# Two-layer convolution-attention block on Trainium2: the order of 128-row and five-row score products in a tile's attention

## The chip, the cores and the metric

The kernel runs on one core of one Trainium2 chip, in one launch. The metric is the device time of that launch in microseconds (us), the median of several runs. The core's engines are named as the profile names them: PE is TensorE (PEld its weight loads), DVE is VectorE, ACT is ScalarE, POOL is GpSimd, SP is SyncE. PE writes its results into PSUM[...]; DVE and ACT read them from there.

## The reference, cut to what matters

The input `x` is fp32 of shape (2, 256, 64, 64): two images of 256 channels. Layer 0 is group norm, an eight-head attention over all 4096 pixels, and a residual. Layer 1 is group norm, then the sum of a grouped 3x3 convolution and of two local attentions in a row, and a residual. The change is in the first of these two attentions. Cut down, it is:

```python
q = conv1x1(x, conv1_w, conv1_b); k = conv1x1(x, conv2_w, conv2_b); v = conv1x1(x, conv3_w, conv3_b)
pos = tile(conv1x1(loc, convp_w, convp_b))        # loc: two coordinates of each pixel
fq = q * 64 ** (-0.5) + pos
fk = k + pos
# blockify: pixels with the same place inside their 8x8 block form a group; 64 groups an image,
# 64 pixels and 256 channels a group
att = softmax(einsum('bcn,bcm->bnm', blockify(fq), blockify(fk)) * 256 ** (-0.5))
ctx = einsum('bnm,bcm->bcn', att, blockify(v))
feats = relu(conv1x1(ctx, lr_W_w) * scale + shift)
```

The score of a query pixel n and a key pixel m in a group is a product over the 256 channels of `fq` and `fk`. Multiplied out, it has a part that contracts the input with itself through one folded 256x256 matrix, and parts that contain `pos` or a bias. The latter depend on few numbers for each pixel.

## The kernel before, in words

`tile_two_layer_kernel` calls `direct_layers`, which does all the work for one image (b = 0) and then for the other (b = 1). For each image it runs `project0` and `attention0` (layer 0), `layer1_first` (the first attention of layer 1, the subject here) and `layer1_second` (the second attention, `group_attention` again, and the convolution in between).

`layer1_first` first writes the normalised image into `xg`, in the order of groups. The 64 groups are cut into eight tiles t of eight groups, 512 pixels each; `source(t)` is that piece of `xg`, two chunks (c) of 128 channels by 512 pixels. For each tile there is:

- `project` (L1176, ACT copy at L1180): the tile multiplied by the folded matrix, `py`, copied to `y`. It runs two tiles ahead.
- `at_grid` (L1190, DVE at L1195 and L1198), twice an image: five rows for each pixel that hold the position and bias parts, as `queries` and `keys`. Tile t uses five rows from row 32 * (t % 4) of half t // 4.
- `group_attention`, a generator with the tile's softmax. It makes the values `vs` (L1060), and the scores `sp` (L1078 and L1084). `sp` is one PSUM bank: 128 partitions, four blocks of 64 columns. Block t of the inner loop, for `par` 0 and 1, holds group 4 * par + t on partitions 64 * par to 64 * par + 63. A group's scores are the sum of two products of 128 rows (c = 0 and 1: `y` against `xg`, L1078) and one product of five rows (`queries` against `keys`, L1084). Then DVE takes the row maximum (`nm`, L1094) and subtracts it (L1096), ACT takes the exponential (L1097), DVE the row sum, its reciprocal and the scaling (L1099 to L1101). After the first `yield`, PE transposes the result (`at`, L1106) and DVE spreads it into `bd` (L1115); after the second, PE multiplies it with the values (`pc`, L1124) and ACT writes `feats` (L1137).

The second attention calls the same function with `more=None`: its scores have only the 128-row products, 16 a tile.

The order on PE is written by hand (`tc.manual_schedule(engines={E.PE})`): the scores and values of tile t come first, then half the projection of tile t + 2, the transposes of tile t - 1, the other half, and the products `pc` of tile t - 1. In the last two tiles, which have nothing left to project, the generator stops once more behind the scores, and the transposes of tile t - 1 follow directly. The order on the other engines in this part is the planner's.

Beside the first image's attention DVE makes the convolution's weights in `conv_weights` (L888 to L936, tiles named `prep`): a long chain of scale-and-add steps of 128x256 (L917), in two halves. The second half's input `wx` is loaded by POOL's queue (L909) into room that the first half frees. The results go to memory from SP's queue (L930), and `fetch_conv_weights` loads them back as `wf` (L946) for the first convolution in `layer1_second`, where PE transposes them (L955). ACT fills `xp`, the padded image for the convolution, at the end of the stage (L1295), and POOL transforms it (`col`, L982, and `v`, L986) for the convolution's products (`mm`, L996).

Of the kernel before, what the change touches and what calls it, by code (L numbers as in the profile page):

```python
# [22 lines left out]
KC = C // P  # L23
# [17 lines left out]
def direct_layers(ctx: ExitStack, tc: tile.TileContext, a: dict, out: bass.AP, bad: bass.AP):  # L41
# [3 lines left out]
    nc = tc.nc  # L45
# [13 lines left out]
    def w4(shape, name, dtype=F32):  # L59
        return work.tile(shape, dtype, tag="w4", name=name)  # L60

    def bank(shape, name):
        return psum["ps"].tile(shape, F32, tag="bank", name=name)
# [983 lines left out]
    def group_attention(nm, q, k, tokens, wv, out, busy=False, apart=False, more=None, between=None):  # L1047

        vs = w4([P, 4, C], f"vs_{nm}")

        def values(half):
            pv = bank([P, 2, C], f"pvs_{nm}_{half}")
            for i in range(2):
                for c in range(KC):
                    nc.tensor.matmul(  # L1060
                        pv[:, i, :], tokens(c, 2 * half + i), wv[:, c, :], start=c == 0, stop=c == KC - 1
                    )
            dst = vs[:, 2 * half : 2 * half + 2, :]
            if half == 0 or busy or apart:
                nc.scalar.copy(dst, pv)
            else:
                nc.vector.tensor_copy(dst, pv)

        first = apart or more and more[2]
        if first:  # L1070
            values(0)

        sp = bank([P, 4, 64], f"sp_{nm}")
        for t in range(4):
            for c in range(KC):
                for par in range(2):
                    n0 = (4 * par + t) * 64
                    nc.tensor.matmul(  # L1078
                        sp[64 * par : 64 * par + 64, t, :], q[:, c, n0 : n0 + 64], k[:, c, n0 : n0 + 64],
                        start=c == 0, stop=not more and c == KC - 1,  # L1080
                    )
            for par in range(2 if more else 0):
                n0 = (4 * par + t) * 64
                nc.tensor.matmul(  # L1084
                    sp[64 * par : 64 * par + 64, t, :], more[0][:, n0 : n0 + 64], more[1][:, n0 : n0 + 64], start=False, stop=True
                )
        if more and more[3]:
            yield
        if not first:
            values(0)  # L1090
        if not apart:
            values(1)
        nm4 = small.tile([P, 4], F32, tag="nm4", name=f"nm4_{nm}")
        nc.vector.tensor_reduce(nm4, sp, AX.X, ALU.max, negate=True)  # L1094
        e = small.tile([P, 4, 64], F32, tag="e", name=f"e_{nm}")
        nc.vector.tensor_tensor(e, sp, nm4.unsqueeze(2).to_broadcast([P, 4, 64]), ALU.add)  # L1096
        nc.scalar.activation(e, e, AF.Exp, scale=SC1)  # L1097
        den = small.tile([P, 4], F32, tag="den", name=f"den_{nm}")
        nc.vector.tensor_reduce(den, e, AX.X, ALU.add)  # L1099
        nc.vector.reciprocal(den, den)  # L1100
        nc.vector.tensor_tensor(e, e, den.unsqueeze(2).to_broadcast([P, 4, 64]), ALU.mult)  # L1101

        yield
        at = bank([P, 2, 2, 64], f"at_{nm}")
        for u in range(2):
            nc.tensor.transpose(  # L1106
                at[:, u].rearrange("p a i -> p (a i)"),
                e[:, 2 * u : 2 * u + 2, :].rearrange("p t j -> p (t j)"), ident,
            )

        bd = bds[turn[0] % 2]
        turn[0] += 1
        for tt in range(2):
            rows = slice(64 * tt, 64 * tt + 64)
            nc.vector.tensor_copy(  # L1115
                bd[rows, :, tt, :].rearrange("p (a u) i -> p u a i", a=2), at[rows]
            )
        if apart:
            values(1)
        yield  # L1120
        for m in range(KC):
            pc = bank([P, T], f"pc_{nm}_{m}")
            for w in range(4):
                nc.tensor.matmul(  # L1124
                    pc[:, w * P : (w + 1) * P], vs[:, w, m * P : (m + 1) * P],
                    bd[:, w].rearrange("p a i -> p (a i)"), start=True, stop=True,
                )
            out(m, pc)
            if m == 0 and between:
                between()  # L1130
# [11 lines left out]
    def layer1_first(b, xts, put, check, st):  # L1142
# [102 lines left out]
        with tc.manual_schedule(engines={E.PE}):  # L1245

            before = None
            for t in range(NT + 1):
                parts = None
                if t < NT:  # L1250
                    def to_feats(m, pc, t=t):
                        kept["feats"] = bn_relu(
                            feats[m][:, :, t, :].rearrange("p o e -> p e o"),
                            pc.rearrange("p (e o) -> p e o", e=8), V_LR, m,
                        )

                    rows = slice(HD0 * (t % 4), HD0 * (t % 4) + AT)
                    parts = group_attention(
                        f"lr_{b}_{t}", tiles.pop(t), source(t),
                        lambda c, w, t=t: source(t)[:, c, w * P : (w + 1) * P], wts["w3"], to_feats, b == 0,  # L1260
                        more=(queries[rows, t // 4, :], keys[t // 4][rows, :], t == 0, t >= NT - 2),
                    )
                    next(parts)
                    if t == 3:
                        at_grid(1)
                for m in range(KC):
                    if t + 2 < NT:
                        project(t + 2, m, slice(1 if t == 0 else 0, KC))
                    if before:
                        next(before, None)  # L1270
                    if m == 0 and NT - 2 <= t < NT:
                        next(parts)
                before = parts
# [5 lines left out]
    def layer1_second(b, xts, feats, mean, rstd, shift, pacc, following):  # L1279
# [59 lines left out]
        for t in range(NT):  # L1339
# [25 lines left out]
            with tc.manual_schedule(engines={mybir.EngineType.PE}):  # L1365
# [17 lines left out]
                def to_res(m, pc, res=res):  # L1383
# [4 lines left out]
                    )  # L1388

                parts = group_attention(  # L1390
                    nt, q, k, lambda c, w, f=f: f[c][:, w * P : (w + 1) * P], wts["fv"], to_res, apart=t + 1 < NT,
                    between=lambda: next(then) if b == 0 and t == NT - 1 else None,
# [630 lines left out]
```

## Time and profile before

| | |
|---|---|
| median of three runs | 3069.78 us (3066.59 to 3073.84) |
| the profiled execution's own time | 3067.66 us |
| its span | 3065.9 us |
| PE busy | 2986.3 us (97%) |
| DVE busy | 2456.4 us (80%) |
| ACT busy | 2340.4 us (76%) |
| POOL busy | 832.6 us (27%) |
| score products of 128 rows in the first attention (L1078, `sp_lr`) | 512 records, first at 1161.5 us, last at 2761.1 us |
| score products of five rows (L1084, `sp_lr`) | 256 records, first at 1161.9 us, last at 2761.4 us |

The span is what the profiler saw of the program. The first attention stands at about 1161 to 1248 us for the first image and at about 2684 to 2771 us for the second. The profile writes `_lr` behind the names of the tiles of the first attention and `_sr` behind those of the second. A line of the timeline gives the start, the length, the engine, the line of the kernel, the operation, what is written from what, the shape, the number of records merged (x8), and in brackets the idle time of the engine before it and who ended it. The ends of PE's records are modelled and overlap the next starts, so the distance from start to start tells more than the length.

### The profile page before, as it was taken

To read this page: it belongs to the slowest core of one execution; us is meant where nothing else is said; L and a number is where in the kernel's file an instruction comes from. 1 tells how busy PE (TensorE), PEld (TensorE's weight loads), DVE (VectorE), ACT (ScalarE), POOL (GpSimd) and SP (SyncE) were. 2 spreads that over 40 slices of the span, in tenths; PEclk is the share of its full clock that TensorE was granted. 3 is DMA by queue.
4 is the path that set the end of the run, shared out by engine and by line. 5 is a ranking of instruction groups with operands and counts; after the bars stand their busy time and mean duration, and the time that the engine had idled before them with its cause. 6 is when DMAs were issued, how large, how long until landed. Compare 5 with 4: busy or idle time off the path is not lost. (4 is left out here: it accounts for less than half of the span.)

```text
span 3065.9 us, 63941 instructions
## 1 busy us (share of the span) xinstructions
PE 2986.3 (97%) x25129; PEld 1863.2 (61%) x25129; DVE 2456.4 (80%) x3122; ACT 2340.4 (76%) x3266; POOL 832.6 (27%) x918
## 2 busy tenths in 40 slices
PE   7999999999999999999989999999999999999998
PEld 4565566665556556677755655566555565576765
DVE  4698998989899999856556989989989999835543
ACT  2699999999999983622227999999999999734333
POOL 1122222222223240155301222322222222306440
PEclk9999999999999999999999999999999999999999
DMA  7968789787897661220159688797788976700000
GB/s 259 278 133 179 153 161 177 152 167 161 172 185 160 141 135 32 86 118 28 45 195 271 129 177 163 159 182 145 172 166 170 183 147 128 169 4 4 21 15 22
DMA packets 244148, 425.01 MB, mean 139 GB/s; under 512 B 98888, under 2 KB 109948, under 8 KB 241660
## 3 DMA queue, kind: packets, MB, share of 16 engines
q0 software_dynamic: 94720, 237.57, 40.1%
q1 hardware_dynamic: 148972, 182.99, 21.6%
q8 instruction: 199, 3.26, 0.4%
q14 instruction: 113, 0.93, 0.1%
q10 hardware_dynamic: 144, 0.26, 0.0%
HBM read 119.55 MB, written 68.39 MB: 61 GB/s over the span
## 5 line engine op out<-in xcount | busy, mean ns | idle before, releaser
L551 ACT ACTIVATE es<-ring 128x512 f32<-128x512 f32 (+2 forms) x1572 | 1203.4, 904 | 29.6 <-PE ring L545 21.7
L545 PE MATMUL ring<-q,k 128*128 128x512 f32 x4096 | 1082.3, 407 | 10.1 <-ACT v L551 4.8
L597 DVE TENSOR_TENSOR e<-e,es 128x1024 f32<-128x1024 f32 (+1 forms) x956 | 1035.3, 1144 | 23.1 <-ACT es L551 22.6
L545 PEld LDWEIGHTS ring<-q,k 128*128 128x128 f32 x4096 | 733.7, 188 | 379.8 <-ACT es L551 114.5
L551 ACT ACTIVATE v<-ring 128x512 f32<-128x512 f32 (+2 forms) x1024 | 780.7, 899 | 23.7 <-PE ring L545 12.8
L560 PE MATMUL av<-es,v 128*32 128x256 f32 (+1 forms) x9684 | 725.9, 389 | 0.0
L597 DVE TENSOR_TENSOR e<-e,v 128x1024 f32<-128x1024 f32 (+1 forms) x636 | 669.3, 1107 | 20.3 <-ACT v L551 19.3
L560 PE MATMUL av<-v 128*32 128x256 f32 (+1 forms) x6188 | 497.9, 389 | 0.0
L560 PEld LDWEIGHTS av<-es,v 128*32 128x32 f32 x9684 | 328.0, 110 | 266.1 <-issue 106.4
L560 PEld LDWEIGHTS av<-v 128*32 128x32 f32 x6188 | 221.2, 109 | 170.8 <-issue 72.4
L996 PE MATMUL mm<-v,wf 128*128 128x256 f32 x1024 | 227.6, 380 | 1.5 <-DVE z L1005 1.5
L607 POOL DMA_DIRECT2D es<-es x118 | 100.7, 853 | 465.7 <-ACT es L551 418.1
L996 PEld LDWEIGHTS mm<-v,wf 128*128 128x128 f32 x1024 | 193.3, 190 | 36.9 <-issue 9.9
L986 POOL TENSOR_TENSOR v<-col 128x512 f32<-128x512 f32 x128 | 165.4, 1319 | 177.7 <-ACT rk_sr L1137 39.3
L1001 ACT COPY z<-mm 128x512 f32<-128x512 f32 x32 | 18.7, 586 | 182.7 <-PE mm L996 182.7
L607 POOL DMA_DIRECT2D acc<-es x118 | 118.4, 1009 | 112.4 <-ACT es L551 49.3
L605 POOL DMA_DIRECT2D es<-es x20 | 11.4, 569 | 491.8 <-ACT es L551 405.6
L607 POOL DMA_DIRECT2D es<-v x72 | 61.4, 852 | 290.4 <-ACT v L551 278.0
L1002 DVE TENSOR_TENSOR z<-z,mm 128x512 f32<-128x512 f32 x32 | 22.0, 687 | 138.5 <-ACT z L1001 138.1
L607 POOL DMA_DIRECT2D v<-es x112 | 115.0, 1027 | 19.3 <-ACT es L551 11.2
L607 POOL DMA_DIRECT2D acc<-v x78 | 74.6, 957 | 78.1 <-DMA acc<-es 30.9
L982 POOL TENSOR_TENSOR col<-xp 128x1152 f32<-128x1152 f32 x32 | 69.6, 2175 | 62.1 <-DVE xp L1415 50.8
(254 smaller groups left out, 2680.0 us busy)
## 6 DMA issues: line engine op xcount, KB each, us to landing
acc<-es POOLq DMA_DIRECT2D x128, 512.0 KB, 6.4
acc<-v POOLq DMA_DIRECT2D x84, 512.0 KB, 6.2
es<-es POOLq DMA_DIRECT2D x138, 256.0 KB, 4.3
v<-es POOLq DMA_DIRECT2D x132, 256.0 KB, 5.2
k<-wk_halves SPq DMA_DIRECT2D x64, 512.0 KB
q<-wq_halves SPq DMA_DIRECT2D x256, 128.0 KB
v<-v POOLq DMA_DIRECT2D x90, 256.0 KB, 5.0
es<-v POOLq DMA_DIRECT2D x84, 256.0 KB, 3.9
```

The source lines that it names most:

```text
L545: touch(nc.tensor.matmul(sc[:, i, :], held["k", g // 2][:, j * P : (j + 1) * P], held["q", g, u // 2][:, u % 2, :], start=True, stop=True, ...
L551: nc.scalar.activation(dst, sc, AF.Exp, scale=SC0), set(range(at % BANKS, at % BANKS + m))
L560: note(nc.tensor.matmul(dst[HD0 * u : HD0 * u + HD0, n], lhs, rhs(u)[:, n], start=start, stop=stop))
L597: nc.vector.tensor_add(dst[:, s, :], dst[:, s, :], src)
L605: nc.gpsimd.dma_start(out=dst, in_=src)
L607: nc.gpsimd.dma_start(out=dst, in_=src, accum_op=ALU.add)
L982: (nc.gpsimd.tensor_add if plus else nc.gpsimd.tensor_sub)(col, cols(one), cols(two))
L986: (nc.gpsimd.tensor_add if plus else nc.gpsimd.tensor_sub)(dst, rows(one), rows(two))
L996: nc.tensor.matmul(mm[:, m, r, :], wf[:, k, 4 * r + q, m * P : (m + 1) * P], v[r // 2][:, r % 2, k, :], start=k == 0, stop=k == KC - 1,)
L1001: nc.scalar.copy(z[:, 1], mm[:, :, 1, :])
L1002: nc.vector.tensor_add(z[:, 0], z[:, 1], mm[:, :, 0, :])
```

## The change

For the first attention (`more` given), a tile's 16 products of 128 rows are all issued first, and its eight products of five rows behind them. Before, each of the four blocks had its four 128-row products and then its two five-row products, and was complete before the next block began. Now the sums of all four blocks stay open at once in the bank. The flags follow that: only the first product of block 0 for each `par` carries `start`, the later blocks' first products do not, and `stop` is set on the five-row products of the last block. For the second attention (`more` not given) order and flags stay as they were.

```diff
         sp = bank([P, 4, 64], f"sp_{nm}")
+        def place_of(t, par):
+            return sp[64 * par : 64 * par + 64, t, :], slice((4 * par + t) * 64, (4 * par + t) * 64 + 64)
+
         for t in range(4):
             for c in range(KC):
                 for par in range(2):
-                    n0 = (4 * par + t) * 64
+                    dst, n = place_of(t, par)
                     nc.tensor.matmul(
-                        sp[64 * par : 64 * par + 64, t, :], q[:, c, n0 : n0 + 64], k[:, c, n0 : n0 + 64],
-                        start=c == 0, stop=not more and c == KC - 1,
+                        dst, q[:, c, n], k[:, c, n], start=c == 0 and (t == 0 or not more),
+                        stop=not more and c == KC - 1, skip_group_check=bool(more),
                     )
-            for par in range(2 if more else 0):
-                n0 = (4 * par + t) * 64
-                nc.tensor.matmul(
-                    sp[64 * par : 64 * par + 64, t, :], more[0][:, n0 : n0 + 64], more[1][:, n0 : n0 + 64], start=False, stop=True
-                )
+        if more:
+            for t in range(4):
+                for par in range(2):
+                    dst, n = place_of(t, par)
+                    nc.tensor.matmul(
+                        dst, more[0][:, n], more[1][:, n], start=False, stop=t == 3, skip_group_check=True
+                    )
         if more and more[3]:
             yield
```

## The prediction

> **What bounds the kernel now.** I read the page first: its head and the busy time of each engine.
>
> ```profile
> span 3065.9 us, 63941 instructions
> PE 2986.3 (97%) x25129; PEld 1863.2 (61%) x25129; DVE 2456.4 (80%) x3122; ACT 2340.4 (76%) x3266; POOL 832.6 (27%) x918
> ```
>
> That is an average, so I looked next at the busy time of the two stretches in which the changed code runs, one for each image (b = 0 and b = 1). The columns are length, then PE, PEld, DVE, ACT, POOL.
>
> ```profile
> 1161.00:1244.00 83.00, 83.00 (x691) 61.76 (x690) 73.66 (x199) 35.35 (x51) 2.87 (x7) 1.00 0.18 49
> 2684.00:2767.00 83.00, 83.00 (x692) 61.78 (x691) 28.39 (x66) 31.31 (x43) 0.83 (x6) 1.00 0.02 6
> ```
>
> PE is never idle in either, so a microsecond saved on PE counts, as long as nobody else is nearly as full. In the second image nobody is (DVE 28 of 83). In the first DVE is (74 of 83): it computes the convolution's folded weights (`prep`, L915 to L928) in the same stretch. That difference decides the size of the gain.
>
> "Busy" does not mean well used. The timeline of PE for the scores of one tile (start, length, instruction):
>
> ```profile
> 1179.36 0.45 PE L1078 MATMUL sp_lr<-xg,y 128*64 128x64 f32 x8
> 1179.74 0.33 PE L1084 MATMUL sp_lr<-keys,at 5*64 5x64 f32 x4
> 1180.00 0.45 PE L1078 MATMUL sp_lr<-xg,y 128*64 128x64 f32 x8
> 1180.38 0.33 PE L1084 MATMUL sp_lr<-keys,at 5*64 5x64 f32 x4
> 1180.64 0.45 PE L1078 MATMUL sp_lr<-xg,y 128*64 128x64 f32 x8
> 1181.02 0.33 PE L1084 MATMUL sp_lr<-keys,at 5*64 5x64 f32 x4
> 1181.28 0.45 PE L1078 MATMUL sp_lr<-xg,y 128*64 128x64 f32 x8
> 1181.66 0.33 PE L1084 MATMUL sp_lr<-keys,at 5*64 5x64 f32 x4
> 1181.92 3.72 PE L1060 MATMUL pvs_lr<-wt_w,xg 128*128 128x256 f32 x16
> ```
>
> Each fp32 product leaves two records, so x8 is four products. Read the starts, since lengths overlap. A visit of four 128-row products takes 0.38 us until the five-row ones begin; a visit of two five-row products takes 0.26. The tile's scores take 1181.92 - 1179.36 = 2.56 us. The second attention does the same 16 products of 128 rows with nothing between them, which gives the price of an unbroken run:
>
> ```profile
> 1410.88 1.15 PE L1078 MATMUL sp_sr<-rk_sr,rq_sr 128*64 128x64 f32 x32
> 1411.96 7.17 PE L996 MATMUL mm<-v,wf 128*128 128x256 f32 x32
> ```
>
> 16 products in 1.08 us. Twelve more than a visit of four cost 0.70 us, 0.058 each; so the visit of four holds 4 x 0.058 = 0.23 of work and **0.15 us of starting and stopping**.
>
> **The Trainium skill.** "TensorEngine Tiling (Array Packing)", Key Properties, says that a change of tiling mode, as opposed to a change of tile, drains the TensorE. A product of 128 rows and one of five rows at a 32-row position are different modes. The trace agrees with some such cost: 0.15 us a visit, against 0.058 a product. "PSUM — Partial Sum Buffer", The four PSUM rules, says that of several sums open in one bank and quadrant only the first matmul may carry the start flag; the others find their bits cleared and overwrite. The new flags do this, so no clearing instruction is added; no run here tests that rule yet. The same page, Engine vs sequencer instructions, says that VectorE's queue is strictly first in, first out; the DVE waits below, with `prep` work queued behind them, look so.
>
> **The change part by part.** Counts first: 16 + 8 products per tile before and after, same shapes. No DMA and no instruction of DVE, ACT, POOL or SP is added, removed or moved.
>
> *Order on PE.* Per tile, four visits of 128 rows and four of five rows become one and one: six of eight changes of mode go. New time: 1.08 for the run of 16, then one visit of eight five-row products. Their price in a run is not in the trace. Taking 0.058 also for these (their weight load, median 130 ns, is no longer than the 138 of the others), today's visit of two holds 0.26 - 0.12 = 0.14 of overhead, and the new one takes 0.14 + 8 x 0.058 = 0.60. Sum 1.68, **saving 0.88 us a tile, 7.0 us for each image's eight tiles, 14.0 in all.** Bounds: if each five-row product keeps its present 0.13 even in a run, they take 1.04 and the saving is 0.44 a tile; if further ones were free, 0.26 and 1.22. Dearer than 0.13 I exclude: that price already contains a change of mode for every two products (the tile would lose only above 1.48 / 8 = 0.185 each). Equal load and 64 columns streamed speak for the middle.
>
> *Waits.* The row maximum (L1094) still waits for the last five-row product, now 0.88 earlier. At tile 0 the five-row products wait for `keys` from DVE, done at 1161.71 (start 1160.97, 0.74 long); they now come later, so nothing new waits. The start flags cost nothing: they are a field of instructions that exist.
>
> *Second image.* PE has no wait inside the stretch, and DVE waits 5.2 us at a time for PE's scores. What follows (`bd`, then `feats`, then `xp`, with 1.05 and 2.76 us of PE waits at 2768.53 and 2773.31) is triggered by PE and moves along whole. **7.0 us arrive.**
>
> *First image.* DVE's `prep` chain runs from here to 1293.84, and DVE's queue mixes it with each tile's softmax. What DVE waits for up to 1230 us, from the view of waits (total, times, longest):
>
> ```profile
> DVE nm_lr L1094 <- PE sp_lr L1084: 3.7, 6, 1.2
> DVE bd L1115 <- PE at_lr L1106: 0.8, 3, 0.3
> ```
>
> This is all that DVE can win: when PE is early these 4.5 us vanish. In DVE's timeline they come as 0.23, 1.17, 0.27, 0.48, 0.84, 0.21, 0.48, 0.28, 0.47, and at each the sum so far stays below PE's lead (0.88 times the tiles done). The tile 6 wait of 1.28 does not count, because after it DVE waits 2.7 us for the second half's `wx`, a load that hangs on the first half of `prep`. So from 1237 on DVE is 4.4 us early where PE would be 7.0 early, and PE must meet it at the end of the stage:
>
> ```profile
> 1246.43 2.02 PE L1124 MATMUL pc_lr<-bd,vs_lr 128*128 128x128 f32 x16 [1.76 <-DVE bd L1115]
> ```
>
> That wait for the last `bd` grows from 1.76 to about 4.3. A second gate stands behind it: the first convolution needs `wf`, reloaded when `prep` is finished.
>
> ```profile
> 1297.24 2.76 SPq L946 DMA_DIRECT2D wf<-wf_kept  x4
> ```
>
> The traffic of that reload ends at about 1310.3 in the DMA view, and the last wait before a transpose of it (L955) is at 1311.1: 0.8 us of slack. So even in another DVE order the first image gives at most 4.4 + 0.8 = 5.2. **I take 4.4 us**; bounds 0.8 (the chain gains nothing) and 5.2.
>
> *Sum.* 7.0 + 4.4 = 11.4 us. The profiled execution took 3067.66 (its span 3065.9 and 1.8 around it), so 3056.3; the median shown is 3069.78, 2.1 higher, and against it the forecast is **3058.4**.
>
> **Rivals.**
> 1. *Five-row products stay dear in a run* (0.13 each). For it: no run of them is in the trace. Against: the first of any visit is the slow one for 128 rows too. 3.5 us in the second image; in the first DVE follows PE's smaller lead of 0.44 a tile, 2.6. Total 6.1: 3063.7.
> 2. *The first image is held by `prep`*, since DVE's order or its loads leave it where it is: 7.0 + 0.8 = 7.8, 3062.0. For it: DVE is 89% busy there. Against: its waits are for the very products that get shorter.
> 3. *All arrives*: 14.0, 3055.8. Against: the 0.8 us slack of `wf`, unless `prep` is queued better too.
> 4. *Slower: DVE's queue is ordered anew and badly.* Only PE's order is written by hand here; DVE's is the planner's. If it puts each row maximum of the first image ahead of `prep` work that used to run before it, DVE stands still until the scores come, and `prep`, then `wf`, then PE are late. The 11.4 won must be eaten and 6.1 more lost: 17.5 us over eight tiles, 2.2 a tile, five `prep` operations (0.40 from start to start) put behind each row maximum. Against: counts, shapes and producers are unchanged. From there, 3076 and more.
> 5. *It does nothing*: the gaps are not changes of mode but the wait for the block just written. Then the run of `sp_sr`, which also adds to a block two products later, would show them; it does not. 3069.8.
>
> **Numbers.** First case 0.62, the others 0.13, 0.12, 0.06, 0.03, 0.04. The likeliest gives 3058.4. The range goes from 3053.5 (five-row products almost free, 9.8 + 5.2, less a run's scatter) to 3064 (rivals 1 and 2). The three runs shown spread by 7 us; about 0.2%, 6.1 us, is what a measurement can tell from no change. Case 1 and rivals 2 and 3 pass that, rival 1 about half the time: faster 0.87, same 0.10, slower 0.03.
>
> **What would show it.** Right: per tile one group of 32 records of L1078 and one of 16 of L1084, 1.08 and about 0.60 us from start to start; the 74.7 us of the first image from the first tile's scores to the last's (1161.49 to 1236.21) down by seven savings, to 68.6; DVE's waits for `sp_lr` in the first image near zero; PE's wait for the last `bd` near 4.3 us there and still near 1.0 in the second image. Wrong: a visit of five-row products over 0.8 us; a wait of DVE for the scores as long as before; a PE wait at L955 for `wf`; a different order of `prep` and softmax on DVE.

## The result, and the profile after

The changed kernel takes 3061.3 us in the median (3056.6 to 3062.99) beside 3072.56 us of the kernel before, measured with it: ratio 0.9969, interval 0.9960 to 0.9978. By the ratio that is 9.5 us less (6.8 to 12.3), where the prediction had 11.4; the medians lie 11.3 apart. The median is 2.9 us above the forecast of 3058.4, inside its range of 3053.5 to 3064. Measured twice more the ratio was 0.9977 (0.9968 to 0.9985) and 0.9967 (0.9955 to 0.9978). The profiled execution after took 3062.01 us.

The head and the busy times of the page after:

```profile
span 3060.1 us, 63941 instructions
PE 2979.3 (97%) x25129; PEld 1859.9 (61%) x25129; DVE 2455.9 (80%) x3122; ACT 2340.2 (76%) x3266; POOL 832.1 (27%) x918
```

The counts are the same, as a pure reordering must have them. The timeline of PE for the tile that the prediction showed (L1081 and L1089 are the L1078 and L1084 of before):

```profile
1179.69 1.15 PE L1081 MATMUL sp_lr<-xg,y 128*64 128x64 f32 x32
1180.78 0.68 PE L1089 MATMUL sp_lr<-keys,at 5*64 5x64 f32 x16
1181.38 0.92 PE L1060 MATMUL pvs_lr<-wt_w,xg 128*128 128x256 f32 x3
```

Start to start: 1.09 us for the 16 products of 128 rows, 0.60 for the eight of five rows, 1.69 in all (1.68 worked out). What is left of DVE's waits for PE in the first image up to 1226 us (total, times, longest), 4.5 us before:

```profile
DVE nm_lr L1099 <- PE sp_lr L1089: 0.3, 1, 0.3
DVE bd L1120 <- PE at_lr L1111: 0.3, 1, 0.3
```

PE's waits in the first image's stage, 1161 to 1252 us, and then in the second's, 2684 to 2772 us:

```profile
PE pc_lr L1129 <- DVE bd L1120: 4.0, 2, 2.3
PE phq_sr L1354 <- ACT feats L1142: 1.3, 1, 1.3
PE at_lr L1111 <- DVE e_lr L1106: 0.7, 1, 0.7
```

```profile
PE phq_sr L1354 <- ACT feats L1142: 2.8, 1, 2.8
PE pc_lr L1129 <- DVE bd L1120: 1.0, 1, 1.0
```

In the second image PE waits as before (1.05 and 2.76), so all that it saves arrives. In the first it now waits for DVE twice, and for the last softmax as well.

Where the time went, each stretch taken from start to start on PE in the two traces (`phq`, L1354, is PE's first product behind the stage, in the second attention):

| stretch | before | after | difference |
|---|---|---|---|
| up to the first image's first `sp_lr` | 1161.49 | 1163.58 | +2.09 |
| first image: first `sp_lr` to last `pc_lr` visit | 84.94 | 81.43 | -3.51 |
| last `pc_lr` visit to first `phq` | 3.82 | 4.79 | +0.97 |
| first `phq` to the second image's first `sp_lr` | 1434.06 | 1435.43 | +1.37 |
| second image: first `sp_lr` to last `pc_lr` visit | 84.22 | 77.22 | -7.00 |
| from there to the end | 97.34 | 97.68 | +0.34 |

The sum is -5.74 us, the difference of the spans. The second image gives the 7.0 forecast for it. The first gives 3.5 at its last `pc_lr` and 2.5 at `phq`, where 4.4 was forecast. The stretches that run no changed code differ by up to 2.1 us. This is scatter between executions: in three traces of the changed kernel the first `sp_lr` starts at 1163.58, 1163.78 and 1161.29 us. The sum of the two images, 7.0 + 2.5 = 9.5 us, is the ratio's 9.5, but to the tenth that is luck: the interval is 5.5 us wide, and the other two measurements give 7.1 and 10.1.

**Why the first image gives less: DVE's queue.** The timeline of DVE at the end of that stage, kernel after; PE finished the last tile's scores at 1233.98 us:

```profile
1229.67 0.42 DVE L1106 TENSOR_TENSOR e_lr<-e_lr,den_lr 128x256 f32<-128x256 f32 x1
1235.27 0.62 DVE L915 TENSOR_SCALAR prep<-prep 128x256 f32<-128x256 f32 x2 [5.18 <-DMA prep<-in_wx_dram]
1235.80 2.46 DVE L917 SCALAR_TENSOR_TENSOR prep<-prep 128x256 f32<-128x256 f32 x6
1238.17 0.42 DVE L1099 TENSOR_REDUCE nm_lr<-sp_lr 128x4 f32<-128x256 f32 x1
...
1242.03 2.06 DVE L917 SCALAR_TENSOR_TENSOR prep<-prep 128x256 f32<-128x256 f32 x5
1244.01 0.85 DVE L1120 COPY bd<-at_lr 64x256 f32<-64x256 f32 x2
```

DVE stands still for 5.18 us until a part of `wx` has landed. Behind that waiting instruction stand seven more steps of `prep` (one of L915, six of L917), and only then the last tile's row maximum (L1099), whose input has been there for over 4 us; five more steps stand directly ahead of the last `bd`. This is the strict first in, first out of VectorE's queue that the Trainium skill states ("PSUM — Partial Sum Buffer", Engine vs sequencer instructions): the trace shows ready work at 1233.98 that begins at 1238.17. In the kernel before DVE has the same order, in all its 3122 operations; there the last scores were ready at 1238.77, only 0.8 us ahead of the row maximum:

```profile
1236.69 0.62 DVE L915 TENSOR_SCALAR prep<-prep 128x256 f32<-128x256 f32 x2 [2.72 <-DMA prep<-in_wx_dram]
1239.59 0.41 DVE L1094 TENSOR_REDUCE nm_lr<-sp_lr 128x4 f32<-128x256 f32 x1
```

From the end of DVE's wait for the load to the last `pc_lr` visit it is 9.74 us in both kernels (1236.69 to 1246.43, 1235.27 to 1245.01). So the end of this stage follows the landing of the load in both; before, PE's own work was about as late (`rotate_bd_old` below), and now PE is early. POOL's timeline has the loads:

```profile
1220.01 0.75 POOL L909 DMA_DIRECT2D prep<-in_wx_dram  x1 [69.67 <-DVE prep L917]
1229.30 0.75 POOL L909 DMA_DIRECT2D prep<-in_wx_dram  x1 [8.54 <-DMA wf_kept<-prep]
1231.72 0.75 POOL L909 DMA_DIRECT2D prep<-in_wx_dram  x1 [1.67 <-DMA wf_kept<-prep]
```

Each of the three issues brings a third of `wx`. By the kernel's layout the first is rows 8 to 11, into room that DVE has freed; the other two wait until the first half's results have been stored from the room that they share (`new_cols` and rows 0 to 7 of `wx`). DVE starts when the one issued at 1229.30 lands, at 1235.24.

### The profile page after: what moved, and what is told of

Its sections match the earlier page's. It is cut to its first block, busy times and chain, and to the rows that moved or that the text cites. A ratio compares the mean times of both kernels' runs of the same rounds, so it can differ in the third digit from the quotient of the medians.

```text
span 3060.1 us, 63941 instructions
## 1 busy us (share of the span) xinstructions
PE 2979.3 (97%) x25129; PEld 1859.9 (61%) x25129; DVE 2455.9 (80%) x3122; ACT 2340.2 (76%) x3266; POOL 832.1 (27%) x918
## 5 line engine op out<-in xcount | busy, mean ns | idle before, releaser
L605 POOL DMA_DIRECT2D es<-es x20 | 11.4, 569 | 495.2 <-ACT es L551 404.6
```

## The experiments

All numbers of the stages in one table, in us from the first `sp_lr` of the image; the last column is how long PE's granted clock (the share of full clock that the trace gives for a stretch) was at half around the end of the first image's stage (in us, added up from windows of 0.5 us between 1236 and 1258):

| kernel | ratio to before | first image, to last `pc_lr` | to `phq` | second image, to last `pc_lr` | half clock |
|---|---|---|---|---|---|
| before | 1 | 84.94 | 88.76 | 84.22 | 0 |
| after | 0.9969 | 81.43 | 86.22 | 77.22 | 3.4 |
| `new_again` | 0.9977 | 81.67 | 86.18 | 77.23 | 6.8 |
| `after_third` | 0.9967 | 81.46 | 85.65 | 77.23 | 6.8 |
| `img0_only` | 0.9997 | 82.92 | 87.99 | 84.23 | 10.2 |
| `img1_only` | 0.9978 | 85.06 | 89.14 | 77.22 | 6.8 |
| `less_prep_new` | 0.9973 | 80.94 | 84.40 | 77.43 | 0 |
| `rows128_old_order` | single run | 81.45 | 86.33 | 76.08 | 3.4 |
| `two_blocks` | single run | 81.69 | 86.50 | 79.56 | 3.4 |
| `lighter_dve_new` | 0.9974 | 82.85 | 87.75 | 77.22 | 3.4 |
| `no_reload_new` | 0.9943 | 78.07 | 81.89 | 77.23 | 0 |
| `rotate_bd_old` | 0.9998 | 84.58 | 88.77 | 84.22 | 0 |
| `rotate_bd_new` | 0.9962 | 78.26 | 81.92 | 77.23 | 0 |
| `rotate_bd_again` | 0.9952 | 78.23 | 82.46 | 77.23 | 6.8 |

### One image at a time

The new order and flags in the first image alone (`img0_only`, whose edit is shown cut), in the second alone (`img1_only`, the same with `lr_1_`), and the changed kernel once more beside them (`new_again`):

```diff
+        if more and nm.startswith("lr_0_"):
...
+            for t in range(4):
+                for c in range(KC):
...
+            if more:
+                for t in range(4):
+                    for par in range(2):
...
+        else:
+            for t in range(4):
+                for c in range(KC):
...
+                for par in range(2 if more else 0):
```

> The new order for the first image only, the old one for the second. Theory (the first image is gated by DVE's prep chain): from the first sp_lr to phq_sr of the first image PE gains about 2.5 to 4.4 us of the 7.0 that its scores save; its wait for the last bd is over 4 us there, and the second image's stretch keeps its old length. Total 2.5 to 4.5 us faster than the kernel before (ratio 0.9985 to 0.9992). Rival (all arrives): 7.0 us, ratio 0.9977. Rival (wf holds everything): 0.8 us, 0.9997.

> The new order for the second image only. Theory: 7.0 us arrive whole, since only PE is full there: from the first sp_lr to the last visit of pc_lr of the second image 77.2 us against 84.2 before, total ratio 0.9977. Rival (a wait behind PE takes some of it, or the half-clock stretch at its end does): 4 to 5 us, ratio 0.9985.

> The changed kernel once more, on the same chip as the two halves, for a second profile. Theory: the sum of the halves, 9.5 to 11.5 us, ratio 0.9963 to 0.9969. If the halt of PE at the end of the first image lets the clock fall to half (3.4 us, 1.4 us lost by the last pc_lr), that shows again with the 2 us wait before it; if it was chance, that pc_lr visit takes 2.0 us.

Measured: 0.9997 (0.9989 to 1.0005) for the first image alone, 0.9978 (0.9969 to 0.9987) for the second alone, 0.9977 for both. So nearly all of the gain in the runs, 6.8 us of it, is the second image's, as expected of `img1_only`. Two expectations failed: `img0_only` was to reach 0.9985 to 0.9992, and `new_again` 0.9963 to 0.9969. The 0.9997 is the number of the rival "wf holds everything", but not for its reason: the trace has no wait at L955. In it PE gains 2.0 us up to the last `pc_lr` (0.9 of its 82.92 is a wait for `keys` at the first tile), and 10.2 us at half clock around there leave 0.8 at `phq` and nothing at the first transposes of `wf` (`pw`, L955), which come 146.51 us into the stage against 145.21 before. The first image is the one to explain.

### Is it the change of mode?

`rows128_old_order` keeps the order of before, but the position products contract all 128 rows:

```diff
-                        more=(queries[rows, t // 4, :], keys[t // 4][rows, :], t == 0, t >= NT - 2),
+                        more=(queries[:, t // 4, :], keys[t // 4][:, :], t == 0, t >= NT - 2),
```

> The order before the change, in which each of the four blocks has its four products of 128 rows and then its position products; but the position products contract all 128 rows of `queries` and `keys` instead of five (so the scores also contain the position terms of other tiles: other numbers, same counts). Nothing then changes the number of contracted rows inside a tile's scores. Theory (the 0.15 us of each visit is the price of changing between 128-row and five-row products): 24 products in one run, 24 x 0.058 + 0.15 = 1.54 us from the first score product of a tile to its values, against 2.56 before and 1.68 after. Rival (the gaps are waits for the block that was just written): the order of writing is that of before, so it stays near 2.56.

Its timeline of PE for one tile:

```profile
1178.64 0.45 PE L1078 MATMUL sp_lr<-xg,y 128*64 128x64 f32 x8
1178.92 0.29 PE L1084 MATMUL sp_lr<-keys,at 128*64 128x64 f32 x4
1179.04 0.40 PE L1078 MATMUL sp_lr<-xg,y 128*64 128x64 f32 x8
...
1180.19 3.72 PE L1060 MATMUL pvs_lr<-wt_w,xg 128*128 128x256 f32 x16
```

1.55 us against 2.56, with the same order of writing. The position products now contract the rows of other tiles as well, so the scores are other numbers, with the same counts. In the same place two products behind four now take 0.12 (1179.04 - 1178.92), 0.06 each, where two five-row ones took 0.26. The rival, waits for the block just written, is out.

`two_blocks` is the changed kernel with two blocks open at once, that is four visits a tile:

```diff
-        for t in range(4):
+        each = 2 if more else 4
+        for u in range(0, 4, each):
+            for t in range(u, u + each):
+                for c in range(KC):
...
-        if more:
-            for t in range(4):
+            for t in range(u, u + each if more else u):
                 for par in range(2):
```

> The changed kernel with two blocks open at once instead of four: eight products of 128 rows, four of five rows, and the same again; four visits a tile instead of two (after) or eight (before). Theory (0.15 us a visit, 0.058 a product): 1.68 + 2 x 0.15 = 1.98 us a tile, and the second image from its first scores to its last `pc` visit 77.2 + 8 x 0.30 = 79.6 us, against 84.2 before and 77.2 after. Rival (what counts is how many sums are open at once, so that a block is added to only after the other three were written): not on this line; two open sums would give most of the gain, under 1.8, or little of it, over 2.3.

```profile
1177.21 0.69 PE L1083 MATMUL sp_lr<-xg,y 128*64 128x64 f32 x16
1177.83 0.45 PE L1090 MATMUL sp_lr<-keys,at 5*64 5x64 f32 x8
1178.20 0.69 PE L1083 MATMUL sp_lr<-xg,y 128*64 128x64 f32 x16
1178.82 0.45 PE L1090 MATMUL sp_lr<-keys,at 5*64 5x64 f32 x8
1179.19 3.72 PE L1060 MATMUL pvs_lr<-wt_w,xg 128*128 128x256 f32 x16
```

1.98 us, and 79.56 for the second image's stage, as worked out (1.98 and 79.6). A visit costs 0.15 us, whichever its products, and with 8, 4, 2 or 1 visits a tile takes 2.56, 1.98, 1.69 or 1.55. So what counts is the number of visits, not how many sums are open at once. This agrees with the Trainium skill ("TensorEngine Tiling (Array Packing)", Key Properties), where a change of tiling mode drains TensorE; the price, 0.15 us, is from these runs.

The two kernels tell more. PE's own work for eight tiles is 2.3 us longer in `two_blocks` than after, and 1.1 shorter in `rows128_old_order`; the second image's stages show just that (79.56, 77.22, 76.08). The first image's stages are 81.69, 81.43 and 81.45. **There PE's speed no longer matters**, over 3.4 us of its work: something else sets the end. In both kernels the last `pc_lr` again comes 9.74 to 9.75 us behind DVE's wait for the load (1232.43 to 1242.17 and 1234.52 to 1244.27).

### What of DVE?

`less_prep_new` is the changed kernel with ten instead of twelve terms in each of the convolution's folded weights, 36 scale-and-add steps fewer in the two halves:

```diff
-                for i in range(12):
+                for i in range(10):
```

> The changed kernel with two of the twelve scale-and-add steps of each tap left out of the folded convolution weights (36 of 216 operations at L917, 0.40 us each: 7.2 us in each half), so the convolution's weights are other numbers. If DVE's prep chain is what held the first image, PE keeps its 7.0 us there: waits of PE for at_lr and bd below 2 us in sum, first sp_lr to phq_sr about 81 us or less (before: 88.8, changed kernel: 86.2), and the total is 4 to 6 us below the changed kernel. If ACT or PE itself holds it, the total is that of the changed kernel.

Measured: 0.9973 (0.9962 to 0.9985), no more than the change alone, and 84.40 us up to `phq` where about 81 was expected. The load is issued 8.6 us earlier in the stage (57.13 against 65.72) and lands at 1223.72. DVE waits 2.5 us for it, but 10 us ahead of the last tile's scores, so this wait is not what holds the last softmax. Yet the last `pc_lr` comes only 0.5 us earlier; the other 1.3 us that this trace has won at `phq` lie behind it, where this execution has no half clock. DVE's timeline, with the last scores ready at 1233.75:

```profile
1223.74 0.62 DVE L915 TENSOR_SCALAR prep<-prep 128x256 f32<-128x256 f32 x2 [2.51 <-DMA prep<-in_wx_dram]
...
1235.08 1.27 DVE L917 SCALAR_TENSOR_TENSOR prep<-prep 128x256 f32<-128x256 f32 x3
1236.27 0.42 DVE L1099 TENSOR_REDUCE nm_lr<-sp_lr 128x4 f32<-128x256 f32 x1
...
1240.12 2.06 DVE L917 SCALAR_TENSOR_TENSOR prep<-prep 128x256 f32<-128x256 f32 x5
1242.10 0.85 DVE L1120 COPY bd<-at_lr 64x256 f32<-64x256 f32 x2
```

Between the scores and their row maximum DVE makes seven steps of `prep`, all ready by then. Less work for DVE helps little while the queue has such steps ahead of the last softmax.

`lighter_dve_new` gives work of DVE away: the softmax's scaling to ACT, and the sums of rows 0 and 3 in `conv_weights` to POOL:

```diff
+                eng = nc.vector if r in (1, 2) else nc.gpsimd
...
-        nc.vector.tensor_tensor(e, e, den.unsqueeze(2).to_broadcast([P, 4, 64]), ALU.mult)
+        if nm.startswith("lr_0_"):
+            for t in range(4):
+                nc.scalar.activation(e[:, t, :], e[:, t, :], AF.Copy, scale=den[:, t : t + 1])
...
```

> The changed kernel with two pieces of DVE's work given away in the first image's attention: the scaling of the softmax goes to ACT (four operations a tile, 128x64 each), and of the sums in `conv_weights` those of rows 0 and 3 go to POOL. PE's order is untouched. Theory (DVE's queue, with `prep` ahead of the last tile's softmax and the `wx` load in it, keeps PE from the first image's 7.0 us): PE's wait for the last `bd` shrinks from 4.0 us to under 2, and the first image, from its first scores to `phq`, falls from 86.2 to about 83.5 us; the whole is some 2 to 3 us faster than the changed kernel, ratio to before about 0.9965. Rival (not DVE but the clock, which drops at the end of the stage whatever DVE does): the wait may shrink, but a half-clock stretch stays at the seam and the length remains near 86. Second rival (ACT, which also makes the exponentials, becomes late): PE waits for ACT's `e` at the transposes, over 1 us in sum.

Measured: 0.9974 (0.9963 to 0.9985) and 82.85 us up to the last `pc_lr`, 87.75 up to `phq` where 83.5 was expected: my theory was wrong here. DVE's waits for the load shrank to 3.2 us, but it then had ten scale-and-add steps (L917) directly ahead of the last row maximum instead of six, and PE waited longer, also for ACT's scaling (1.2 us), as the second rival had it. The waits of PE in its first image:

```profile
PE pc_lr L1136 <- DVE bd L1127: 4.3, 4, 1.6
PE phq_sr L1361 <- ACT feats L1149: 1.3, 1, 1.3
PE at_lr L1118 <- ACT e_lr L1111: 1.2, 2, 0.6
```

`no_reload_new` leaves out the second half's loads of `wx`:

```diff
-                nc.gpsimd.dma_start(out=wx[:, 4 * q : 4 * q + 4, :], in_=a["wx"][q, m].rearrange("i p c -> p i c"))
+                if m == 0:
+                    nc.gpsimd.dma_start(out=wx[:, 4 * q : 4 * q + 4, :], in_=a["wx"][q, m].rearrange("i p c -> p i c"))
```

> The changed kernel without the second half's loads of `wx` (L909): the second half of `conv_weights` uses the first half's numbers, so half of the convolution's weights are other ones. DVE no longer waits for that transfer at L915 (5.2 us in the changed kernel). Theory (the transfer's late landing is what cost the first image most of its gain): PE's wait for the last `bd` falls from 4.0 to under 2.5, no half-clock stretch at the seam, the first image from its first scores to `phq` takes about 84 us instead of 86.2, some 2 us in the whole. Rival (it is the planner's order, which puts work on `prep` ahead of the last tile's softmax, that makes the last `bd` late; without the load there is more such work ready): the wait stays near 4 and the length near 86.

```profile
PE phq_sr L1355 <- ACT feats L1143: 1.8, 1, 1.8
PE pc_lr L1130 <- DVE bd L1121: 1.8, 1, 1.8
```

These are PE's only waits in the first image's stage, and the same two as before the change (1.8 and 1.8). The stage is 6.9 us shorter than before, so nearly the whole of what PE saves arrives, 2 us more than expected. The order on DVE is another one too: without the load `prep` steps fill the time ahead of the last tile, and the row maximum starts 1.8 us behind its scores instead of 4.2. So this run shows that load and queue together are the cause, but not which of the two. Its ratio, 0.9943 (0.9930 to 0.9957), is 17.5 us, more than the 13.9 of the two stages; where the rest comes from is open (half of its convolution's weights are other numbers).

### Mending the queue

The third of `wx` that comes early is rows 8 to 11. `rotate_bd_new` begins the second half's sums with them, and issues what needs the other rows behind the last `bd`:

```diff
-                for i in range(12):
+                for n in range(12):
+                    i = (n + 8 * m) % 12
                     src, s = wx[:, i, :], weff[:, m, i, tap : tap + 1]
-                    if i == 0:
+                    if n == 0:
                         nc.vector.tensor_scalar(acc, src, s, None, ALU.mult)
+                    elif m and n >= 4:
+                        with tc.issue_after(kept["last_bd"].ins):
+                            nc.vector.scalar_tensor_tensor(acc, src, s, acc, ALU.mult, ALU.add)
...
+        if nm == "lr_0_7":
+            kept["last_bd"] = spread
```

> The changed kernel with two edits in the second half of `conv_weights`, both on DVE only: its twelve terms are summed in another order (rows 8 to 11 of `wx` first, whose third of the load is issued about 9 us ahead of the other two), and the terms that need the later thirds are issued only behind the last tile's `bd`. No operation is added or left out. Theory (the load's late landing and the work on `prep` queued ahead of the last softmax cost the first image 4 of its 7.0 us): DVE's idle 5.2 us before the second half are filled, no operation ahead of the last `bd` waits for the late thirds, PE's last wait for `bd` is about 2 us or less, no half-clock stretch at the seam, and the first image from its first scores to `phq` takes 82 to 83 us instead of 86.2; `prep` ends some 4 us earlier, so L955 has no wait; the whole is about 3 to 4 us faster than the changed kernel, ratio to before 0.9940 to 0.9955. Rival (the missing microseconds are not DVE's: PE's clock or its own order): it stays at 86 and 0.997.

> The same two edits on DVE, in the kernel before the change. Theory (before the change PE itself was the bound of the first image, with DVE close behind): little to gain, the first image 88.0 to 88.8 us from its first scores to `phq` against 88.76, ratio to before 0.999 to 1.0; so between this and the kernel with the same edits and the new order lie nearly 7.0 us for each image, 13 to 14 in all, which is what the change is worth where DVE is out of the way. Rival (DVE's queue held the first image before the change too): this kernel gains 2 us or more by itself, and the new order adds under 11.

The timeline of DVE in `rotate_bd_new`, with the last scores ready at 1232.42:

```profile
1230.74 2.46 DVE L921 SCALAR_TENSOR_TENSOR prep<-prep 128x256 f32<-128x256 f32 x6
1233.11 0.42 DVE L1103 TENSOR_REDUCE nm_lr<-sp_lr 128x4 f32<-128x256 f32 x1
...
1239.27 0.85 DVE L1124 COPY bd<-at_lr 64x256 f32<-64x256 f32 x2
1240.15 3.25 DVE L919 SCALAR_TENSOR_TENSOR prep<-prep 128x256 f32<-128x256 f32 x8
```

and of PE:

```profile
1240.27 2.02 PE L1135 MATMUL pc_lr<-bd,vs_lr 128*128 128x128 f32 x16 [1.95 <-DVE bd L1124]
1243.92 3.70 PE L1360 MATMUL phq_sr<-feats,wt_fq 128*128 128x512 f32 x8 [1.64 <-ACT feats L1148]
```

No idle time of DVE is left, the row maximum follows its scores after 0.7 us instead of 4.2, and the stage takes 81.92 us up to `phq`. The load still lands 71.6 us into the stage, as after; it only no longer stands in the way. The two edits, the order of the sums and their place behind the last `bd`, were not tried apart. In the kernel before the same edits bring nothing (0.9998, 0.9989 to 1.0006; 88.77 us). Between the two the new order is worth 6.85 us in the first image and 7.0 in the second by the traces, and 12.1 us by the medians (3069.62 and 3057.56, measured together), where 13 to 14 was expected.

Its median, 3057.56 us, 0.9962 (0.9949 to 0.9976), is the shortest of the versions that compute the whole reference, but it misses the 0.9940 to 0.9955 that was expected, and the interval overlaps that of the changed kernel. It was set beside the changed kernel once more:

> The kernel of `rotate_bd_new` once more, beside the changed kernel on the same chip. Theory: the first image from its first scores to `phq` again near 81.9 us (86.2 in the changed kernel), 3 to 4.5 us faster than the changed kernel in the median. Rival (the 82 us were one lucky execution without a half-clock stretch): near 83.5, and 1.5 to 2 us faster.

> The changed kernel a third time, as the measure of the kernel beside it: ratio to before 0.9965 to 0.998, the first image from its first scores to `phq` 86 us, and a half-clock stretch of 3.4 us or more at its last `pc` visit.

Measured: 3057.58 and 3060.48 us, 0.9952 (0.9938 to 0.9967) and 0.9967 (0.9955 to 0.9978), 2.9 us between the medians, where 3 to 4.5 was expected. The intervals overlap a little, so for the whole kernel the gain over the change is likely but not certain. In the first image's stage it holds: 78.23 us up to the last `pc_lr` against 81.46, and 82.46 up to `phq` against 85.65, with 6.8 us of half clock in both. The rival, a lucky execution without half clock, changes little up to there: with none, `rotate_bd_new` took 81.92. It shows behind `phq`, as the last section tells.

## Why the prediction was right, and which term was off

- **Price of the visits: right.** 1.69 us a tile against 1.68, 77.22 for the second image, exactly 7.0 less. That five-row products cost no more in a run than the others, taken from equal weight loads, held: 0.60 for eight.
- **Second image: right**, all of it arrives, with the two waits behind it as they were.
- **First image, DVE's lead: right.** Forecast 4.4 us from its vanishing waits. The last step of its first half (L928) starts 62.70 us into the stage instead of 67.39, and the late `wx` load is issued at 65.72 instead of 70.45, both 4.7 earlier.
- **First image, what becomes of that lead: the term that was mis-sized.** I let DVE be 4.4 us early "from 1237 on". Between the first half and the last tile lies a load, whose length the prediction took as unchanged. It took 5.94 us from issue to landing instead of 4.71, so it landed 3.5 us earlier, not 4.7, and the last `pc_lr` visit came those 3.5 us earlier, to the hundredth. In the traces of after, `new_again`, `after_third`, `two_blocks` and `rows128_old_order` it lands 71.7 to 71.9 us into the stage, whether it was issued at 65.2 or 67.1. The DMA engines are busy with the stores of the first half and other loads at that time (0.5 to 1.0 of them in each microsecond from 1222 to 1236); whether that holds the load was not tried.
- **Not foreseen: the clock.** Of the 3.5 us one more was lost behind the last `bd`, where PE ran at half clock for 3.4 us: its `pc_lr` visit took 3.46 instead of 2.02, less 0.47 that it then waited less for `feats`. Forecast 4.4, found 3.5 and 2.5; for the kernel after, the bounds, 0.8 and 5.2, held.
- **The signs.** From the first tile's scores to the last's 68.7 us (1163.58 to 1232.29; forecast 68.6). The wait for the last `bd` was forecast at 4.3: it came as 4.0, but over two tiles. No wait at L955.
- **The upper bound: too low for another order on DVE.** 5.2 us was to hold "even in another DVE order". With the queue mended the first image gives 6.85: `prep` then ends 121 us into the stage instead of 130, and the 0.8 us of slack at `wf` does not bind.
- **The rivals.** The first, dear five-row products, and the last, no effect, are out. The third, all arrives, is what the kernel does once DVE's queue is mended. The second, held by `prep`, was half true: not the amount of `prep` held it (`less_prep_new`), but where it stands in the queue. The slower case asked for `prep` steps put behind the row maxima. DVE's operations stand in the same order before and after; the harm was the opposite one, row maxima behind `prep` steps, in an order that was there before, and cost half a gain instead of a loss.

## What to carry to other kernels

Group small TensorE products by their shape, so that each tile changes between 128 contracted rows and few only twice; read the price off the starts of one tile, not off the busy time, which was 97% before and after. Before a gain on one engine is credited to the whole, follow the other engine's queue up to the next load: a lead ends where an instruction waits for a transfer, and everything queued behind that one waits with it. If the gain stops there, taking work off the queue may change little; here moving ready work ahead of the waiting one, and the rest behind the urgent one, brought it back.

## What the runs showed of the hardware

At the end of the first image's stage PE's granted clock falls to half for 3.4, 6.8 or 10.2 us, in steps of 3.41, after stretches in which PE mostly waits. In the kernel after, and then in the kernel before, the windows around the last `pc_lr` (busy times, then PEclk):

```profile
1245.00:1248.00 3.00, 2.99 (x15) 3.00 (x16) 3.00 (x9) 2.25 (x3) 0.00 (x0) 0.55 0.00 0
```

```profile
1245.00:1248.00 3.00, 1.57 (x14) 1.60 (x15) 2.95 (x9) 3.00 (x6) 0.00 (x0) 1.00 0.00 0
```

The Trainium skill ("TensorE: Matmul & The Clock Gate", What's actually happening) describes a clock gate that looks at free-running windows of 3.4 us and halves the clock after an idle one. The steps agree. So does the luck in it: the same kernel showed none of it in `rotate_bd_new` and 6.8 us in `rotate_bd_again`, which came 2.3 us later to `pw` (141.03 us into the stage against 138.76). But no window here was idle from end to end: the drop above begins at about 1245.33, and in the 3.41 us ahead of it PE made two transposes and began its `pc_lr` visit, 0.7 us of work. The stretch appeared at this place in seven of eight traces in which DVE's queue held up a faster PE, and in two of the six others, one of them (`img1_only`) with the order of before in that image.

The traces also tell why it looks like chance. Within a trace the drops start whole multiples of 3.41 us apart. Laid on that grid, the window just ahead of the drop had PE busy for 0.54 to 1.53 us in the nine traces with a drop at this place; in the five without one the least busy window there had 1.64 to 1.98. `img1_only` (1.53, a drop) and the kernel before (1.65, none) run the same order here, so where the grid falls on PE's waits seems to decide. A longer wait leaves less work in some window, which would make the drop likelier. Elsewhere in the same traces drops follow windows with up to 2.9 us of PE's work, so this is a reading of this one place and no threshold of the chip.
